# Fixing the order of the first heads phase of a graph network kernel, with two tap steps a block

## The chip, the core and the metric

The kernel runs on one core of one Trainium2 chip. The metric is the device time of one execution in microseconds (us); lower is better. The engines of the core are TensorE (PE in the profile; its weight loads are PEld), VectorE (DVE), ScalarE (ACT), GpSimd (POOL) and SyncE (SP). SyncE and ScalarE issue DMA transfers, each through a queue of its own.

## The reference

The input x has 128 graphs of 128 nodes and 256 channels, and a 0/1 adjacency matrix for each graph. All is float32. Layer 0 normalises and clips each node, and then has two branches: a pair of convolutions along the nodes, and a message passing step. A gated unit joins them. Layer 1 works on 25 nodes and is not touched by the change. Cut to what matters here:

```python
h = maximum(layernorm(x), 0)
xc = transpose(h)                             # channels x nodes
g = relu(bn1(conv1(xc)))                      # 1 tap: a product with a 256 x 256 matrix
g = bn2(conv2(g))                             # 17 taps along the nodes, 256 x 256 each
x_conv = relu(g + xc)
x_nmp  = (exp(-dist) * adj) @ relu(h @ w_msg.T + b_msg)
x = x + gated_unit(concat(x_conv, x_nmp), h)  # w_ih, w_hh
x = x + layer1(x, adj)                        # five small graph convolutions
```

## The kernel before, in words

The 17-tap convolution is done in the frequency domain. Nodes are cut into two windows of 80 samples; a window has 40 complex frequencies (`NP_`), with the first one holding two real ones. The graphs are worked on in blocks of four (`BB`), 16 blocks to a half, two halves (`NH`). The program has these phases:

1. **Heads of the first half.** Per block: `head_load` brings four graphs (tile `ln`, 512 KB). `head_stats` computes mean and variance on VectorE and the power -1/2 on GpSimd (L192, tile `rs`). `head_norm` normalises on VectorE (L198). `head_turn` transposes on TensorE (L208), clips on ScalarE into `ht` (L209) and stores `ht` for later (L210). `head_conv1` is the one-tap convolution (L222), an add on VectorE (L225) and a clip on ScalarE (L226) into `h1`. `head_spectra` transforms to frequencies (L237); VectorE and ScalarE put the result into the large tile `X` (L243, L245).
2. **Spectra of the taps**, woven into phase 1. `weight_spectra` transforms the taps of 128 input by 64 output channels at a time. There are eight such chunks, each of four *steps* (32 steps in all). A step has 16 small matmuls (L160, 17 rows, 80 columns) into four banks; ScalarE empties three and VectorE one (L168, L166), in the last step of a chunk ScalarE all four. When a chunk is done its 2.5 MB are stored to `vd` (L170), and the taps of the next but one are loaded (L150). `some_spectra(k)` does k steps; it is called twice in each block of `heads`.
3. **Frequencies of the first half** (`spectral`). Frequencies are worked on one after another. A tile `v` with the spectra of two frequencies is loaded from `vd` (L287, three buffers). GpSimd makes the sum `vs` of real and imaginary part (L302, three buffers), TensorE does three products in each frequency (L305, L314; L295 for the first), VectorE and ScalarE combine them into `ys`, which goes to `yd` (L318).
4. **Heads and frequencies of the second half.** The heads' beginning (`heads_begin`: loads, stats, norms and a turn) is called eight frequencies before the end of phase 3.
5. **Everything else** (L394 on), blocks of four graphs again: messages, inverse transform, gated unit, layer 1.

Three things set the order of the work. [...] That order is chosen by the framework's planner, which takes ready instructions by its own model of time and may move an instruction far ahead of its place in the text. Where a block of text stands under `manual_schedule`, the instructions of the named engines (of all, when none is named) keep the order of the text. The kernel before has no such block. It has two tricks that hold the planner back: a one-element-per-row copy from `h1` into the tile of the stats (L185), which ties the stats to the block before, and three one-column copies from `k1` into the tiles of the gate weights (L311), which keep the gate weights behind frequency 20.

PSUM, the accumulator of TensorE, has eight banks of 128 x 512, and all phases take their banks in turn from one pool (`bank`).

The weights of the gated unit (`wih`, `whh`), those of the messages (`wms`, `bms`), `idm` and `fw` are loaded in the text behind phase 3, 2.7 MB in all, and `gate_weights` makes twelve sums of them on GpSimd (L333 to L336).

## Time and profile before

The time before is 1971.03 us (median of three runs, 1967.3 to 1971.71). The profiled execution has a span of 1965.5 us.

| Engine | busy, us | share of the span | instructions |
|---|---|---|---|
| PE (matmuls) | 1910.6 | 97% | 10418 |
| PEld (weight loads) | 1666.5 | 85% | 10418 |
| DVE | 1279.2 | 65% | 3247 |
| ACT | 714.1 | 36% | 1472 |
| POOL | 610.0 | 31% | 684 |

The mean granted clock of TensorE is 0.983 of full speed; full speed is given as 1.00 in the views by window. By phase, from the views by window:

| Phase | from, us | to, us | granted clock | DMA share |
|---|---|---|---|---|
| start, to the first one-tap convolution | 0 | 21.9 | 0.95 | 0.85 |
| first heads, with tap steps | 21.9 | 133.6 | 0.78 | 0.71 |
| first heads, without | 133.6 | 211.7 | 0.93 | 0.61 |
| first frequencies | 211.7 | 321.4 | 0.98 | 0.83 |
| second heads | 321.4 | 427.4 | 1.00 | 0.45 |
| second frequencies | 427.4 | 529.7 | 1.00 | 0.85 |
| everything else | 529.7 | 1965 | 1.00 | 0.35 |

In lines of the profile, `out<-in` names the tile written and those read, `xN` counts instructions, and what stands in square brackets is the time for which the engine sat idle just before, with the instruction or transfer whose end released it. One fp32 matmul of the program gives two records.

### The profile page before, as it was taken

To read this page: it belongs to the slowest core of one execution; us is meant where nothing else is said; L and a number is where in the kernel's file an instruction comes from. 1 tells how busy PE (TensorE), PEld (TensorE's weight loads), DVE (VectorE), ACT (ScalarE), POOL (GpSimd) and SP (SyncE) were. 2 spreads that over 40 slices of the span, in tenths; PEclk is the share of its full clock that TensorE was granted. 3 is DMA by queue.
4 is the path that set the end of the run, shared out by engine and by line. 5 is a ranking of instruction groups with operands and counts; after the bars stand their busy time and mean duration, and the time that the engine had idled before them with its cause. 6 is when DMAs were issued, how large, how long until landed. Compare 5 with 4: busy or idle time off the path is not lost.

```text
span 1965.5 us, 29935 instructions
## 1 busy us (share of the span) xinstructions
PE 1910.6 (97%) x10418; PEld 1666.5 (85%) x10418; DVE 1279.2 (65%) x3247; ACT 714.1 (36%) x1472; POOL 610.0 (31%) x684
## 2 busy tenths in 40 slices
PE   7997999999989999999999999999999999999998
PEld 6887878998878888888878888888878888888887
DVE  5346545765478777777756677777756677777643
ACT  4443212431133333433434433333334434333334
POOL 1002363114423343344322143343322143343300
PEclk9788999999999999999999999999999999999999
DMA  8665688439863323323423533322423533322135
GB/s 325 262 268 192 221 267 299 152 122 304 281 203 83 94 70 85 91 68 81 121 61 100 127 104 89 90 71 72 126 71 91 130 94 97 82 71 61 46 91 148
DMA packets 248853, 265.76 MB, mean 135 GB/s; under 512 B 106850, under 2 KB 223927, under 8 KB 244223
## 3 DMA queue, kind: packets, MB, share of 16 engines
q1 hardware_dynamic: 236767, 196.74, 35.7%
q10 hardware_dynamic: 11936, 67.11, 8.5%
q8 instruction: 83, 1.36, 0.3%
q14 instruction: 67, 0.55, 0.1%
HBM read 178.66 MB, written 85.14 MB: 134 GB/s over the span
## 4 chain that ended last, share of the span: by engine, by line
PE 89%; DMA 4%; DVE 3%; POOL 1%; ACT 1%; issue 1%; SPq 0%; ACTq 0%; POOLq 0%; DVEq 0%
PE bank L572 44%; PE bank L314 7%; PE bank L478 5%; PE bank L222 5%; PE bank L891 5%; PE bank L831 5%; PE bank L305 3%; PE bank L237 3%; PE bank L460 3%; PE bank L524 3%; PE bank L463 1%; PE bank L511 1%; PE bank L810 1%; PE bank L742 1%; PE bank L208 1%; DVE st L187 1%
## 5 line engine op out<-in xcount | busy, mean ns | idle before, releaser
L572 PE MATMUL bank<-t,sw 128*128 128x256 f32 x1152 | 290.7, 379 | 0.0
L585 POOL TENSOR_TENSOR u<-u,m 128x256 f32<-128x256 f32 x128 | 92.7, 724 | 594.8 <-ACT m L583 536.2
L572 PEld LDWEIGHTS bank<-t,sw 128*128 128x128 f32 x1152 | 215.5, 190 | 29.6 <-issue 2.3
L572 PE MATMUL bank<-t,wih 128*128 128x256 f32 x768 | 197.2, 379 | 0.0
L572 PEld LDWEIGHTS bank<-t,wih 128*128 128x128 f32 x768 | 143.4, 190 | 19.3 <-DVE u L590 0.5
L302 POOL TENSOR_TENSOR vs<-v 128x512 f32<-128x512 f32 x78 | 101.1, 1315 | 141.3 <-DMA v<-vd 99.2
L222 PE MATMUL bank<-wc,ht 128*128 128x256 f32 x512 | 128.7, 408 | 12.8 <-ACT ht L209 11.4
L222 PEld LDWEIGHTS bank<-wc,ht 128*128 128x128 f32 x512 | 104.2, 208 | 29.8 <-ACT ht L209 12.9
L478 PE MATMUL bank<-wms,ht 128*128 128x259 f32 x512 | 122.3, 381 | 0.0
L300 DVE SCALAR_TENSOR_TENSOR s<-X 128x256 f32<-128x256 f32 x78 | 51.8, 666 | 98.9 <-PE bank L314 98.5
L572 PE MATMUL bank<-t,whh 128*128 128x256 f32 x384 | 114.4, 379 | 0.0
L891 PE MATMUL bank<-w,hh 128*125 128x256 f32 (+9 forms) x480 | 113.5, 380 | 0.9 <-DVE hh L836 0.9
L572 PE MATMUL bank<-xn,wih 128*128 128x256 f32 x384 | 114.2, 379 | 0.0
L572 PE MATMUL bank<-xc,wih 128*128 128x256 f32 x384 | 114.2, 379 | 0.0
L572 PE MATMUL bank<-ht,whh 128*128 128x256 f32 x384 | 109.8, 379 | 0.0
L478 PEld LDWEIGHTS bank<-wms,ht 128*128 128x128 f32 x512 | 97.2, 190 | 14.6
L831 PE MATMUL bank<-ax,w 128*128 128x500 f32 (+8 forms) x416 | 107.0, 396 | 0.4 <-DMA w<-in_w_dram 0.4
L192 POOL TENSOR_TENSOR rs<-ve,mhalf 128x4 f32<-128x4 f32 x32 | 32.3, 1008 | 232.0 <-DVE ve L190 232.0
L590 DVE TENSOR_TENSOR u<-bank,u 128x256 f32<-128x256 f32 x128 | 53.7, 420 | 73.5 <-PE bank L572 73.5
L482 ACT ACTIVATE msg<-msg 128x512 f32<-128x512 f32 x64 | 40.3, 630 | 167.4 <-DVE msg L479 162.0
L891 PEld LDWEIGHTS bank<-w,hh 128*125 128x125 f32 (+9 forms) x480 | 84.3, 178 | 19.1 <-DVE hh L836 1.3
L237 PE MATMUL bank<-fd,h 128*128 128x160 f32 x512 | 85.3, 323 | 8.4 <-DVE X L243 3.7
(192 smaller groups left out, 4255.2 us busy)
## 6 DMA issues: line engine op xcount, KB each, us to landing
v<-vd SPq DMA_DIRECT2D x80, 512.0 KB
vd<-sp ACTq DMA_DIRECT2D x8, 2560.0 KB
yd<-ys ACTq DMA_DIRECT2D x40, 512.0 KB
w<-in_w_dram SPq DMA_DIRECT2D x40, 512.0 KB
htd<-ht ACTq DMA_DIRECT2D x32, 512.0 KB
ht<-htd SPq DMA_DIRECT2D x32, 512.0 KB
ym<-yd SPq DMA_DIRECT2D x32, 512.0 KB
xt<-in_xT_dram SPq DMA_DIRECT2D x32, 512.0 KB
```

The source lines that it names most:

```text
L222: nc.tensor.matmul(pv[:, bb, :], ht[:, c, b * N:(b + 1) * N], wc1[:, c, :], start=c == 0, stop=c == C - 1)
L237: nc.tensor.matmul(ps[:, bb * 2 * LW:(bb + 1) * 2 * LW], h1[:, 2 * h + bb, c * P:(c + 1) * P], fd, start=True, stop=True)
L302: nc.gpsimd.tensor_tensor(vs, vr, vi, op=ALU.add)
L305: nc.tensor.matmul(p1[:, :D], a[:, c], vs[:, c], start=c == 0, stop=c == C - 1)
L314: nc.tensor.matmul(ps[:, k * D:(k + 1) * D], u[:, c], w[:, c], start=c == 0, stop=c == C - 1)
L460: nc.tensor.matmul(ps[:, b * N:(b + 1) * N], ym[:, b, o * P:(o + 1) * P], idm, start=b == 0, stop=False)
L478: nc.tensor.matmul(ps[:, :D + 3], ht[:, c, b * N:(b + 1) * N], wms[:, c, :], start=c == 0, stop=c == C - 1)
L524: nc.tensor.matmul(ps[:, b * N:(b + 1) * N], msg[:, b, c * P:(c + 1) * P], e[:, b, :], start=True, stop=True)
L572: nc.tensor.matmul(ps, w, d, start=n == 0, stop=n == len(pairs) - 1)
L585: nc.gpsimd.tensor_tensor(got["u4"], got["u2"], got["m5"], op=ALU.add)
L831: nc.tensor.matmul(pv[:, q - q0, :], w1s[k5 + g][:, c, q * P:(q + 1) * P], xv[:, c], start=c == 0, stop=c == C - 1)
L891: nc.tensor.matmul(ps[:n1, :D], hh[:, q, at:at + n1], w2s[k5 + g][:, q, :], start=q == 0, stop=q == HID // P - 1)
```

## The change

The heads of the first half, with the tap steps, get the order of the text on every engine (`ws.enter_context(tc.manual_schedule())`). SyncE and GpSimd get it from there to the end of the frequency phases (`order`, closed behind the loop over the halves). To suit this, the text is put in the order in which it is to run: the loads of the constants are split off, the start is written out with five tap steps in it, `heads_begin` serves the second half only, and `heads` does one tap step at each of its two places instead of two, so that the steps spread over some 14 blocks instead of seven. The stats of the first half are no longer tied to `h1`, and the copies of L311 are gone. The loads of the gate's weights go to frequency 4 of the first half (`gate_loads`) and the gate sums to frequency 20 (`NP_ // 2`); both stand in the text in front of that frequency's own instructions.

```diff
@@ heads @@
             if i + 3 < i1:
-                head_stats(wk, i + 3, h1s[i])
-
-    def spectral(bp, X, h, near_end):
+                head_stats(wk, i + 3, h1s[i] if h else None)
+
+    def spectral(bp, X, h, amid):
 
         for p0 in range(0, NP_, 4):
-            if p0 == NP_ - 8:
-                near_end()
+            amid.get(p0, lambda: None)()
...
-                if h == 0 and p == NP_ // 2:
-
-                    for t in sw:
-                        nc.gpsimd.tensor_copy(t[:, 0, 1, 0:1], k1[:, 0:1])
...
+        order = es.enter_context(ExitStack())
+        order.enter_context(tc.manual_schedule(engines={nc.sync.engine, nc.gpsimd.engine}))
         with ExitStack() as ws:
+
+            ws.enter_context(tc.manual_schedule())
...
-            taps = [taps_load(wp, *todo[k], nc.sync, split=1 if k else 4) for k in range(2)]
-            head_stats(hk, 0)
-            head_norm(0)
+            taps = [taps_load(wp, *todo[0], nc.sync, split=4)]
...
-            some_spectra(3)
+            constant_loads()
+            head_load(xk, ahead, 1, nc.sync)
+            taps.append(taps_load(wp, *todo[1], nc.sync))
+            for k in range(2, ahead):
+                head_load(xk, ahead, k, nc.sync)
+            head_stats(hk, 0)
+            some_spectra()
+            head_norm(0)
+            some_spectra()
+            head_turn(hk, 0)
             constants()
-            heads_begin(hk, xk, ahead, 0)
-            some_spectra(3)
-            heads(hk, xk, ahead, X, 0, lambda: some_spectra(2))
+            some_spectra()
+            head_stats(hk, 1)
+            some_spectra()
+            head_norm(1)
+            head_stats(hk, 2)
+            some_spectra()
+            heads(hk, xk, ahead, X, 0, some_spectra)
             while spectra or todo:
                 some_spectra()
...
+        def gate_loads():
+            nc.sync.dma_start(idm, io["idm"])
+            nc.sync.dma_start(wms, io["wms"].rearrange("(c p) o -> p c o", p=P))
+            nc.sync.dma_start(bms, row("bms", D + 3))
+            nc.sync.dma_start(fw, row("fw", 5))
+            nc.sync.dma_start(wih, io["wih"].rearrange("(c p) o -> p c o", p=P))
+            nc.sync.dma_start(whh, io["whh"].rearrange("(c p) o -> p c o", p=P))
+
+        amid = {4: gate_loads, NP_ // 2: gate_weights, NP_ - 8: lambda: heads_begin(hk, xk, 3, 1)}
         for h in range(NH):
             if h:
                 heads(hk, xk, 3, X, h, lambda: None)
-            spectral(bp, X, h, lambda: heads_begin(hk, xk, 3, h + 1) if h + 1 < NH else None)
-            if h == 0:
...
-                gate_weights()
+            spectral(bp, X, h, {} if h else amid)
+        order.close()
```

More of the change, by code (lines that the diff above doesn't have):

```diff
@@ L112, in gnn_kernel, with constant_loads @@
     brz = cst.tile([P, 4], F32)
-    def constants():
+    def constant_loads():
         nc.sync.dma_start(vec, io["vec"])
@@ L117, in constants @@
         nc.sync.dma_start(fd, io["fd"])
+    def constants():
         for j, v0 in enumerate((V_BN1, V_BN2)):
@@ L249, in heads_begin @@
         i = h * NBH
-        for k in range(1 if h == 0 else 0, ahead):
-            head_load(xk, ahead, i + k, nc.scalar if h else nc.sync)
-        for k in range(1 if h == 0 else 0, 3):
+        for k in range(ahead):
+            head_load(xk, ahead, i + k, nc.scalar)
+        for k in range(3):
             head_stats(wk, i + k)
@@ L383, in gnn_kernel @@
                 heads(hk, xk, 3, X, h, lambda: None)
-            spectral(bp, X, h, lambda: heads_begin(hk, xk, 3, h + 1) if h + 1 < NH else None)
-            if h == 0:
-                nc.sync.dma_start(idm, io["idm"])
-                nc.sync.dma_start(wms, io["wms"].rearrange("(c p) o -> p c o", p=P))
-                nc.sync.dma_start(bms, row("bms", D + 3))
-                nc.sync.dma_start(fw, row("fw", 5))
-                nc.sync.dma_start(wih, io["wih"].rearrange("(c p) o -> p c o", p=P))
-                nc.sync.dma_start(whh, io["whh"].rearrange("(c p) o -> p c o", p=P))
-                gate_weights()
+            spectral(bp, X, h, {} if h else amid)
+        order.close()
     wk = ctx.enter_context(tc.tile_pool(name="wk", bufs=1, reuse_waits="tile"))
```

## The prediction

> **What bounds the kernel now.** I read the page first. Its chain of waits gives 89% of the span to TensorE (PE), so a gain must come from PE idling or running slowly. Section 2 has the granted clock below 9 tenths only in its first slices, and PE's busy digits dip there too. So I cut the span by phase with the windows view (columns: busy us and instruction counts of PE, weight loads, VectorE (DVE), ScalarE (ACT) and GpSimd (POOL), then clock, DMA share, GB/s).
>
> ```profile
> 0.00:21.90 21.90, 13.06 (x208) 12.45 (x208) 11.32 (x48) 9.80 (x23) 4.53 (x14) 0.95 0.85 275
> 21.90:133.60 111.70, 99.26 (x1080) 85.78 (x1081) 46.71 (x149) 48.76 (x137) 7.04 (x7) 0.78 0.71 280
> 133.60:211.70 78.10, 64.71 (x386) 59.01 (x384) 53.44 (x189) 30.81 (x90) 13.90 (x13) 0.93 0.61 218
> 211.70:321.40 109.70, 105.57 (x484) 92.38 (x485) 49.20 (x79) 15.99 (x42) 59.37 (x52) 0.98 0.83 275
> 321.40:427.40 106.00, 104.64 (x636) 96.24 (x636) 76.39 (x266) 48.97 (x139) 16.69 (x16) 1.00 0.45 157
> ```
>
> The first half's heads end at 211.7 us. The second half's heads, the same work without tap steps, take 106.0 us at full clock. The tap steps (L160) explain part of the difference: in the timeline two of them (64 records) take 2.03 us at full clock, so 32 are worth 32 x 1.02 = 32 us. 106 + 32 + about 20 for the start is 158; some 53 us are lost. The PE timeline shows where:
>
> ```profile
> 96.79 2.03 PE L160 MATMUL bank<-gt,w 17*128 17x80 f32 x64
> 98.86 1.09 PE L208 MATMUL bank<-ident,ln 128*128 128x128 f32 x8
> 99.89 3.05 PE L160 MATMUL bank<-gt,w 17*128 17x80 f32 x64
> 103.96 1.53 PE L237 MATMUL bank<-fd,h 128*128 128x160 f32 x8 [1.03 <-DVE sp L166]
> 106.24 2.47 PE L237 MATMUL bank<-fd,h 128*128 128x160 f32 x8 [0.75 <-DVE X L243]
> 108.51 5.26 PE L222 MATMUL bank<-wc,ht 128*128 128x256 f32 x16
> ...
> 159.46 5.04 PE L222 MATMUL bank<-wc,ht 128*128 128x256 f32 x14 [10.08 <-ACT ht L209]
> ...
> 170.83 1.04 PE L208 MATMUL bank<-ident,ln 128*128 128x128 f32 x8
> 171.71 2.34 PE L237 MATMUL bank<-fd,h 128*128 128x160 f32 x16
> 173.88 3.62 PE L222 MATMUL bank<-wc,ht 128*128 128x256 f32 x16
> ...
> 282.55 2.08 PE L305 MATMUL bank<-vs,X 128*128 128x256 f32 x4 [4.10 <-POOL vs L302]
> ```
>
> A block with four steps takes 16.9 us (96.79 to 113.70); a bare block 6.50 (170.83 to 177.34: L208 0.87, L237 2.17, L222 3.45 by starts). Four steps add 4.1, so 6.3 us a block are lost: L237 and L222 run slowly, and two gaps. The clock explains the slowness:
>
> ```profile
> 98.17:101.58 3.41, 3.37 (x70) 3.01 (x66) 2.35 (x10) 3.38 (x11) 0.50 (x1) 1.00 0.11 8
> 101.58:105.00 3.42, 2.35 (x35) 2.04 (x35) 2.18 (x6) 1.49 (x6) 0.51 (x1) 1.00 0.97 372
> 105.00:108.41 3.41, 2.66 (x11) 2.29 (x10) 0.56 (x2) 1.68 (x7) 0.00 (x0) 0.50 1.05 450
> ```
>
> After a stretch of steps and transposes the clock is halved for two such windows. ACT is also full in the first one (3.38 of 3.41 us): it empties three of a step's four banks. The second loss is the 10.08 us gap at 159.46. Its cause stands in POOL's timeline:
>
> ```profile
> 134.90 1.01 POOL L192 TENSOR_TENSOR rs<-ve,mhalf 128x4 f32<-128x4 f32 x1 [15.90 <-DVE ve L190]
> 154.98 1.26 POOL L302 TENSOR_TENSOR vs<-v 128x512 f32<-128x512 f32 x1 [19.07 <-DMA v<-vd]
> 156.19 1.02 POOL L192 TENSOR_TENSOR rs<-ve,mhalf 128x4 f32<-128x4 f32 x1
> ```
>
> The next phase's first sum (L302) stood ahead of a head's power (L192) in POOL's queue and waited 19 us for spectra that were still being stored; the norm, transpose and convolution of that head waited behind it.
>
> [...] every spell of half clock is a multiple of 3.41 us. [...] rows x columns / 128 of the matmul records that start in a window (L160 10.6, L208 128, L237 160, L222 256; sixteen L222 make 4096). Windows that lost the clock had 1247, 1396 and 1556 (from 84.52, 101.58, 118.65); ones that kept it 1513 and 1597 (from 115.24, 98.17). [...]
>
> **The change part by part.**
>
> *Two steps a block, text order.* A block becomes L222, step, L208, step, L237. Its activity is 4096 + 1024 + 2560 + 64 x 10.6 = 8,360 units. Step, transpose, step last 1.02 + 0.87 + 1.02 = 2.9 us, shorter than a window, and hold 1,700 units by themselves: the clock stays whole. PE's floor is 6.50 + 2.04 = 8.5 us. The others have room: DVE two adds 1.3, two bank copies 0.9, norm 1.4, X copies 1.1, stats 2.3: 7.0; ACT two ReLUs 1.2, 6.25 copies at 0.35 are 2.2, two transposes' ReLUs 1.2, X copies 1.0, DMA issues 0.6: 6.2. Laying these out in text order against the eight banks, I find one wait: ACT does L226 first, which stands behind DVE's stats, so step two gets its banks some 0.5 us late. I take 9.1 us a block (bounds 8.6 and 10.5). Removing the copy that ties stats to h1 (L185, 0.2 us) is inside this.
>
> *DMA in this stretch.* Two blocks move 2.56 MB of spectra, 1 MB of taps and 2 x 1 MB of input and ht: 5.6 MB in 18.2 us, 305 GB/s. The trace reaches 450. A tap load goes out behind a 2.56 MB store and has four steps, 18 us, until it is used; 13.4 us were seen for it in the chain. Hidden, with little to spare.
>
> *Start.* Constants in text order put a serial chain on DVE (POOL's two powers at 0.7 each), but five steps instead of six precede the first L222, and vec is issued before the second tap tile. Before it started at 22.1; I take 21, at half clock (5.3 us), as before.
>
> *Sum of the heads.* 21; block 0 without L237 8.3 gives 29.3; twelve blocks at 9.1 give 138.5; block 13 with one step 7.7; block 14 6.5; block 15 5.6; last L237 2.2; X copies 1: 161.5. Before 211.7: **50 us less**. The last store of spectra goes out near 146, lands 9.7 later (chain of before) and the first v 3 us after that, 159: just hidden. POOL's order takes L302 out of the way of L192.
>
> *Gate loads at p = 4.* 2.7 MB, which before ran at 166 to 205 where DMA was idle, now stand between v loads on SyncE, and the second half's three inputs (1.5 MB) fall in the same stretch. v takes 1 MB per two frequencies and yd 0.5: 1.5 MB per 5.18 us, 300 GB/s[...]. From 156 the queue has 0.5 + 1 + 2.7 + 1 MB, plus up to 1.5, before the third v tile is there: 15 to 20 us, 171 to 176, plus the 1.3 us of L302; PE wants it near 173. Cost 0 to 6, I take 3 and, for one window of half clock, 1.5.
>
> *Gate weights at p = 20.* Twelve POOL operations in one piece: eight took 272.10 to 280.29, 1.02 each, so 12.3, plus L302 1.3. POOL is about 8.5 us ahead there (three vs buffers, 2.59 us a frequency): PE waits 5.1 against 4.10 before, each with a window of half clock. Cost 1 (bounds 0 and 5).
>
> *The rest* (SyncE and POOL in text order in the second heads and second frequency phase; the one-element copies L311 gone) I cost at nothing: there v's loads already followed the inputs, PE is 100% busy, and the next phase's loads began only after the last v at 516.
>
> **Sum.** 1971.0 - 50 + 4.5 + 1 = 1926.5; I say **1927 us**.
>
> **Rivals.** (a) *Banks or taps bind*: ACT's in-order work delays each second step by 2 us more, or taps come late. Block 10.9, 12 x 1.8 = 22 less gain: 1949. For it: ACT was full in the window above; against: it then had four steps' copies, now two. (b) *The clock still drops*: half of today's 6.3 us for half of the steps, 3.2 us a block, 12 x 3.2 = 38, and 5 more at start and end: 1970, no change. Against: 1,700 units in 2.9 us. (c) *Slower*: as (b), and the frequency phase becomes DMA-bound[...] and the POOL piece 5 more: about 1984. For it: DMA's share is 0.92 to 0.96 in slices of that phase. Against: the v tiles prefetch ahead.
>
> **How the numbers follow.** Forecast 0.68, (a) 0.18, (b) 0.05, (c) 0.06, and 0.03 for a still larger gain (block 8.6, nothing given back: 1915 or less). The range 1908 to 1955 holds the forecast and (a), and leaves (b) and (c) out. Faster 0.90: forecast, (a), the larger gain and a sliver of (b); same 0.04; slower 0.06.
>
> **What would show it.** Right: blocks near 9 us with clock 1.00 from about 28 us on, no POOL L302 among the L192 of the first half, frequency phase starting near 162, lasting 112 to 118, a PE gap of about 5 us at a POOL piece of twelve. Wrong: half clock recurring between 30 and 150, PE idle before L160 on ACT sp or on tap DMA, or PE waits on vs by v's DMA in many places.

## The result and the profile after

The changed kernel takes 1946.61 us (median of four runs, 1941.89 to 1952.97) against 1971.37 for the kernel before in the same comparison (1967.3 to 1971.94). The ratio is 0.9881, 95% interval 0.9848 to 0.9914: faster clear of the noise, by about 25 us (1.2%) and not by 44. The profiled execution has a span of 1942.6 us.

First the span by phase, in the view by windows of the changed kernel (columns as before). Its phases begin at 21.0, 168.5, 296.4, 402.1 and 504.9.

```profile
0.00:21.00 21.00, 12.92 (x176) 11.92 (x176) 9.41 (x36) 7.73 (x17) 3.88 (x14) 1.00 0.86 295
21.00:168.50 147.50, 143.51 (x1500) 126.18 (x1497) 100.50 (x317) 80.49 (x217) 16.11 (x16) 1.00 0.83 297
168.50:296.40 127.90, 109.62 (x484) 93.93 (x485) 58.54 (x109) 16.19 (x43) 63.43 (x53) 0.93 0.79 256
296.40:402.10 105.70, 104.33 (x634) 95.69 (x634) 78.67 (x264) 48.88 (x139) 16.88 (x16) 1.00 0.53 175
402.10:504.90 102.80, 102.80 (x478) 90.35 (x478) 47.64 (x79) 15.11 (x41) 47.12 (x39) 1.00 0.84 280
```

From 24.8, where the profile's clock record begins, the first heads run at full clock to their end, and PE is busy for 143.5 of their 147.5 us. (Their first convolution, at 21.04, took 5.57 us, later ones 3.62.) They end at 168.5 instead of 211.7. But the first frequency phase now takes 127.9 us where it took 109.7: PE has the same work there and idles for 18 us, and the clock fell to 0.93. So 43 us came in and 18 went back. The three phases behind it (105.6, 102.8 and 1437.8 us) are within 2 us of before (105.4, 102.9, 1435.8).

The PE timeline of the changed kernel, one block of the heads (the one-tap convolution is now L223, the transposes L209, the spectra L238, the steps L162):

```profile
48.96 3.62 PE L223 MATMUL bank<-wc,ht 128*128 128x256 f32 x16
52.50 1.13 PE L162 MATMUL bank<-gt,w 17*128 17x80 f32 x32
53.57 1.09 PE L209 MATMUL bank<-ident,ln 128*128 128x128 f32 x8
54.59 1.18 PE L162 MATMUL bank<-gt,w 17*128 17x80 f32 x32
55.70 2.44 PE L238 MATMUL bank<-fd,h 128*128 128x160 f32 x16
57.98 0.38 PE L223 MATMUL bank<-wc,ht 128*128 128x256 f32 x1
```

It is 9.02 us long (48.96 to 57.98) with no gap in it. Blocks of 9.0 and 9.8 us alternate; in the longer ones the first step stops after four of its 32 records until DVE's second add (L226) of that block is done, at 62.38 in the next block. The step takes 1.9 us there (61.53 to 63.43) instead of 1.1. What the first frequency phase lost stands in three places of the same timeline (L295 is the first frequency, L305 and L310 the products of the others):

```profile
164.43 0.81 PE L238 MATMUL bank<-fd,h 128*128 128x160 f32 x4 [1.27 <-ACT h L227]
166.13 1.90 PE L238 MATMUL bank<-fd,h 128*128 128x160 f32 x12 [0.90 <-ACT h L227]
...
173.02 2.90 PE L295 MATMUL bank<-v,X 128*128 128x256 f32 x6 [3.40 <-issue]
...
226.42 1.03 PE L310 MATMUL bank<-v,X 128*128 128x256 f32 x4
236.59 2.08 PE L305 MATMUL bank<-vs,X 128*128 128x256 f32 x4 [9.15 <-POOL vs L302]
...
275.25 1.10 PE L305 MATMUL bank<-vs,X 128*128 128x256 f32 x4 [3.02 <-DVE ys L311]
```

Two waits on `vs`, of 1.2 and 1.4 us, are the rest of the 18 us. After each of the two larger gaps the first matmuls are slow: the clock is halved for 6.8 us from 171.6 and for 10.2 us from 229.6, the only such spells before the last phase. DVE's timeline explains the first place:

```profile
162.69 0.43 DVE L188 BATCH_NORM_STATS2 st<-ln 128x6 f32<-128x256 f32 x1 [4.56 <-DMA ln<-in_x_dram]
163.04 0.67 DVE L226 TENSOR_TENSOR h<-bank,bnr 128x512 f32<-128x512 f32 x1
...
172.04 0.43 DVE L188 BATCH_NORM_STATS2 st<-ln 128x6 f32<-128x256 f32 x1 [3.37 <-DMA ln<-in_x_dram]
172.38 0.54 DVE L244 COPY X<-bank 128x160 f32<-128x160 f32 x2
```

Stats of the *second* half (L188) stand in DVE's queue ahead of the last block's add (L226) and of its last copies into `X` (L244), and wait for inputs that were only issued at 155 to 164. Under the planner, which still orders DVE behind the heads, they had moved up from frequency 32. The chain of waits has "DMA ln<-in_x_dram" for 7.27 us at 155.40. POOL's timeline has the second place:

```profile
167.21 1.27 POOL L302 TENSOR_TENSOR vs<-v 128x512 f32<-128x512 f32 x1 [19.82 <-DMA v<-vd]
...
219.90 2.49 POOL L302 TENSOR_TENSOR vs<-v 128x512 f32<-128x512 f32 x2 [2.99 <-DMA v<-vd]
222.35 1.18 POOL L329 TENSOR_TENSOR sw<-wih 128x384 f32<-128x384 f32 x1
...
234.33 0.99 POOL L332 TENSOR_TENSOR sw<-whh,sw 128x384 f32<-128x384 f32 x1
235.28 4.92 POOL L302 TENSOR_TENSOR vs<-v 128x512 f32<-128x512 f32 x4
```

The first line is the wait that used to stand in front of a head's power. It is still 19.8 us long, but nothing is queued behind it. The twelve gate sums run from 222.35 to 235.28 in one piece. PE had sums `vs` for 5 us more (to 227.4), then it waited. The third place is DVE's again: norms of the second half, ahead of the combining of `ys` (L311), waited for POOL's power (5.7 us to 265.6, 0.9 to 269.9). Three of them then began together with a sum `vs` on POOL and took 1.35 us each instead of 0.41, as in e2 below.

### The profile page after: what moved, and what is told of

Its sections match the earlier page's. It is cut to its first block, busy times and chain, and to the rows that moved or that the text cites. A ratio compares the mean times of both kernels' runs of the same rounds, so it can differ in the third digit from the quotient of the medians.

```text
span 1942.6 us, 29909 instructions
## 1 busy us (share of the span) xinstructions
PE 1897.4 (98%) x10418; PEld 1652.1 (85%) x10418; DVE 1288.1 (66%) x3247; ACT 713.2 (37%) x1459; POOL 608.8 (31%) x681
## 4 chain that ended last, share of the span: by engine, by line
PE 89%; DVE 4%; DMA 3%; POOL 2%; issue 1%; SPq 0%; ACT 0%; POOLq 0%; DVEq 0%; ACTq 0%
PE bank L586 43%; PE bank L310 5%; PE bank L492 5%; PE bank L905 5%; PE bank L845 5%; PE bank L223 4%; PE bank L238 3%; PE bank L538 3%; PE bank L474 3%; PE bank L305 3%; PE bank L162 2%; PE bank L477 1%; PE bank L525 1%; DMA v<-vd 1%; PE bank L209 1%; PE bank L824 1%
## 5 line engine op out<-in xcount | busy, mean ns | idle before, releaser
L223 PE MATMUL bank<-wc,ht 128*128 128x256 f32 x512 | 118.6, 385 | 1.4 <-ACT ht L210 1.4
L223 PEld LDWEIGHTS bank<-wc,ht 128*128 128x128 f32 x512 | 96.6, 193 | 15.0 <-ACT ht L210 2.8
L193 POOL TENSOR_TENSOR rs<-ve,mhalf 128x4 f32<-128x4 f32 x32 | 32.3, 1011 | 208.9 <-DVE ve L191 208.9
L307 ACT COPY k<-bank 128x256 f32<-128x256 f32 x78 | 29.0, 372 | 185.6 <-PE bank L305 76.2
```

Source lines behind the costliest of these rows:

```text
L223: nc.tensor.matmul(pv[:, bb, :], ht[:, c, b * N:(b + 1) * N], wc1[:, c, :], start=c == 0, stop=c == C - 1)
```

## The experiments

In all of them a phase is measured as above, from the first one-tap convolution or frequency product to the next. The table has what is compared. Each ratio is to the kernel before as measured beside that run (medians 1968.5 to 1972.3 us), so ratios compare better than medians. The three columns of phases are of one profiled execution each. As e8 will show, the same text of the first heads can end 11 us later in one execution than in another, so a few us in these columns need a cause in the trace.

| kernel | median us (range) | ratio to before, interval | heads end at | first frequencies | second heads |
|---|---|---|---|---|---|
| before | 1971.37 | | 211.7 | 109.7 | 105.4 |
| changed | 1946.61 (1941.9–1953.0) | 0.9881 [0.9848, 0.9914] | 168.5 | 127.9 | 105.6 |
| e1 sums spread | 1939.36 (1938.1–1941.6) | 0.9840 [0.9820, 0.9860] | 169.3 | 118.8 | 105.6 |
| e2 gate in second heads | 1937.97 (1935.7–1949.7) | 0.9843 [0.9816, 0.9870] | 169.6 | 114.8 | 110.9 |
| e3 inputs later | 1945.92 (1943.5–1949.4) | 0.9873 [0.9852, 0.9895] | 169.6 | 132.9 | 105.6 |
| e7 both | 1937.02 (1933.0–1939.6) | 0.9826 [0.9804, 0.9848] | 165.2 | 116.3 | 110.9 |
| e4 four steps | 1957.67 (1951.2–1958.6) | 0.9926 [0.9906, 0.9947] | 188.2 | 122.6 | 105.6 |
| e5 planner in the heads | 1988.30 (1983.1–1989.4) | 1.0087 [1.0070, 1.0103] | 216.0 | 125.9 | 105.6 |
| e6 two queues alone | 1954.48 (1950.6–1956.3) | 0.9917 [0.9902, 0.9933] | 195.5 | 111.5 | 105.6 |
| e8 all spread | 1924.27 (1922.9–1935.5) | 0.9781 [0.9758, 0.9804] | 176.1 | 113.0 | 105.6 |
| e9 steps apart | 1942.00 (1940.6–1949.8) | 0.9860 [0.9837, 0.9882] | 169.1 | 124.8 | 105.6 |
| e12 sums behind a copy from `X` | 1942.76 (1937.0–1949.1) | 0.9860 [0.9823, 0.9897] | 180.1 | 114.6 | 113.8 |
| e13 sums behind the norms | 1935.81 (1931.2–1941.6) | 0.9817 [0.9792, 0.9843] | 180.2 | 114.9 | 105.6 |
| e10 spread, steps apart | 1923.08 (1919.3–1925.9) | 0.9758 [0.9736, 0.9779] | 164.4 | 110.6 | 105.6 |

### What the first frequency phase gives back

**e1: the gate sums one a frequency.** The twelve sums are no longer in one piece: from frequency 20 on, each frequency makes one.

```diff
             for p in range(p0, p0 + 4):
+                if h == 0 and p >= NP_ // 2:
+                    next(sums, None)
...
             tt(s3, a11, a21, op=ALU.subtract)
+            yield
...
-        amid = {4: gate_loads, NP_ // 2: gate_weights, NP_ - 8: lambda: heads_begin(hk, xk, 3, 1)}
+        sums = gate_weights()
+        amid = {4: gate_loads, NP_ - 8: lambda: heads_begin(hk, xk, 3, 1)}
```

> The twelve gate sums one to a frequency from 20 to 31 instead of in one piece at 20; the loads stay at 4. Theory A (the piece itself stops PE for 9.2 us and costs a cold window): the first frequency phase falls from 127.5 to 114 to 117 us, no PE wait on vs over 2 us behind frequency 20, about 1934 us. Rival R (v's transfers are late anyway, the piece only covers it): the phase falls by less than 4 us, 1943 us or more.

Measured: the 9.15 us gap and the half clock behind it are gone, and the phase is 118.8 instead of 127.9 us, a little over the theory's 114 to 117. So the piece of twelve cost 9.1 us: the gap, less small waits that stay (up to 2.7 us), and the slow matmuls behind it. The half clock at the phase's start stays (6.8 us from 172.7), and one of 3.4 us comes at 258.0. The total is 1939.36, 7.3 us less, where the theory had about 1934. The second frequencies took 106.0 us in the profiled execution instead of 102.8, with one wait of 2.2 us for `vs`.

**e2: gate loads and gate sums out of the phase.** The loads stand behind the first half's `v` loads, the sums in the second half's heads, one at each of the two places of a block.

```diff
-        amid = {4: gate_loads, NP_ // 2: gate_weights, NP_ - 8: lambda: heads_begin(hk, xk, 3, 1)}
+        sums = gate_weights()
+        amid = {NP_ - 8: lambda: heads_begin(hk, xk, 3, 1)}
...
             if h:
-                heads(hk, xk, 3, X, h, lambda: None)
+                gate_loads()
+                heads(hk, xk, 3, X, h, lambda: next(sums, None))
```

> Gate loads behind the first half's frequencies on SyncE, the twelve sums one at a time in the second half's heads. Theory A: as spreading alone, and 1 to 4 us more where the loads stood between v's: first frequency phase 111 to 115, second heads longer by at most 1, 1930 to 1934 us. Rival R (the transfers bind): over 8 us better than spreading alone, 1926 us or less.

Measured: the phase is 114.8 us, 4.0 less than with the sums spread; that much at most is what the loads at frequency 4 cost, since e1 also had the half clock at 258.0, worth up to 1.7 us (half of its 3.4). But the second heads went from 105.6 to 110.9, where the theory allowed 1 us, and the total is that of e1. Blocks with sums take up to 7.7 us there instead of 6.5, with PE waiting for `ht`. POOL itself isn't late: its power (L193) still waits 4.64 us for DVE in such a block. DVE is. First the same norms in DVE's timeline of the changed kernel, then DVE's of e2, then POOL's of e2:

```profile
321.54 1.38 DVE L199 TENSOR_SCALAR ln<-ln,mv,rs 128x256 f32<-128x256 f32 x4 [1.12 <-POOL rs L193]
```

```profile
319.82 2.80 DVE L199 TENSOR_SCALAR ln<-ln,mv,rs 128x256 f32<-128x256 f32 x4 [1.12 <-POOL rs L193]
```

```profile
319.76 1.00 POOL L329 TENSOR_TENSOR sw<-whh 128x384 f32<-128x384 f32 x1
320.83 0.99 POOL L331 TENSOR_TENSOR whh<-whh 128x384 f32<-128x384 f32 x1
```

The four norms of a block together take twice as long while the two sums run: 2.80 us instead of 1.38. By single records, the two norms that begin together with a sum (within 0.07 us) take 1.08 and 1.15 us and end 0.15 us behind that sum, the other two 0.40 us each as usual, and the sums keep their 1.0 us. The sums start when the power is done, and so do the norms: the place was an unlucky one. What holds the norms up there isn't shown; two later runs, e12 and e13, test whether it is the meeting.

**e3: the second half's inputs later**, loaded by SyncE at frequency 16 and not by ACT's queue.

```diff
-        for k in range(ahead):
-            head_load(xk, ahead, i + k, nc.scalar)
...
-        amid = {4: gate_loads, NP_ // 2: gate_weights, NP_ - 8: lambda: heads_begin(hk, xk, 3, 1)}
+        amid = {4: gate_loads, NP_ // 2: gate_weights, 16: lambda: [head_load(xk, 3, NBH + k, nc.sync) for k in range(3)],
+                NP_ - 8: lambda: heads_begin(hk, xk, 3, 1)}
```

> Only the second half's first three inputs moved: from ScalarE's queue, where the planner issues them at 155 us, to SyncE's at frequency 16. Theory A (VectorE's stats of these inputs stand ahead of the last block's h1 and X copies and wait for the transfer): the first L295 comes 3 to 4 us earlier (about 165), the gap of 3.4 us behind it goes, 1937 to 1940 us. Rival R (the end of the heads waits for the last spectra and v): first L295 stays near 168, 1945 us or more.

Measured: the total, 1945.92, is no better than the changed kernel's, and the heads end at 169.6, as the rival had it. Yet the theory was right about the end of the heads: from the last convolution's start to the first frequency product it now takes 7.8 us instead of 11.2, so the stats are gone from there. It doesn't show in the heads' end, because this execution lost the clock twice among the steps (3.4 us each at 85.0 and 105.5, two blocks of 11.4 us instead of 9.8), and its block 0 was 1.0 us longer. In the first frequency another operation has taken the stats' place. DVE's timeline of e3, then PE's:

```profile
168.67 0.56 DVE L244 COPY X<-bank 128x160 f32<-128x160 f32 x2 [0.53 <-PE bank L238]
176.18 0.16 DVE L438 TENSOR_REDUCE fmx<-fw 128x1 f32<-128x5 f32 x1 [6.96 <-DMA fw<-in_fw_dram]
...
176.51 0.55 DVE L244 COPY X<-bank 128x160 f32<-128x160 f32 x2
```

```profile
177.16 2.90 PE L293 MATMUL bank<-v,X 128*128 128x256 f32 x6 [5.23 <-ACT fex L442]
```

A reduction over the five weights `fw` of a later phase (loaded with the gate's) stands before the last copies into `X` and waits 7 us for its small load, which is queued on SyncE behind `v`. PE waits 5.2 us for those copies (the view names ACT's `fex`, but the matmul reads `X`, whose copy ended at 177.06), and the phase takes 132.9 us. An early load lets the planner bring its reader forward; there were two such loads here, and one taken away left the other.

**e7: e2 and e3 together.** Its edit is the sum of theirs.

> Inputs late and gate loads and sums in the second heads, together. Theory A: the two savings add, first frequency phase 106 to 110 from about 165 us, 1922 to 1927 us. Rival R: no better than the better of the two alone.

Measured: the heads end at 165.2 (the last block's convolution starts at 157.4 in both this and the changed kernel, so the blocked DVE cost 3.3 us there), and the 3.4 us gap in the first frequency is gone. But the total, 1937.02, is no better than e2's, as the rival had it and not the theory, and the first frequencies take 116.3 us. The second heads still lose 5.3 us to the sums. `v` comes 3.7 us late once, at 207; three inputs were issued at once ahead of it, which I take to be the cause. A wait of 3.0 us on DVE's norms, as at 275 in the changed kernel, comes at 255, with 6.8 us of half clock.

**e12 and e13: the sums of e2 at another moment of the block.** In both, six blocks make two sums each, and a one-element copy on POOL in front of the two reads something that is written late. In e12 that is `X`, in e13 the last column that the block's norms write. The edit of e12 on e2, and that of e13 on e12:

```diff
-                heads(hk, xk, 3, X, h, lambda: next(sums, None))
+                heads(hk, xk, 3, X, h, two_sums)
...
+        def two_sums():
...
+            if odd or not 2 <= n < 8:
+                return
...
+            nc.gpsimd.tensor_copy(sw[k][:, 0, j, 0:1], X[:, C - 1, NP_ - 1, 1, HG + (n - 2) * BB:HG + (n - 2) * BB + 1])
+            next(sums)
+            next(sums)
```

```diff
-            if odd or not 2 <= n < 8:
+            if not odd or not 2 <= n < 8:
...
-            nc.gpsimd.tensor_copy(sw[k][:, 0, j, 0:1], X[:, C - 1, NP_ - 1, 1, HG + (n - 2) * BB:HG + (n - 2) * BB + 1])
+            nc.gpsimd.tensor_copy(sw[k][:, 0, j, 0:1], xs[NBH + n + 2][:, BB - 1, D - 1:D])
```

> The run with the gate loads and sums in the second heads, changed in one point: in six of its blocks the two sums stand behind a one-element copy from X, which lets them start when ScalarE has written its last spectra of that block, some 1.3 us after the power, when the block's norms on VectorE are done. Theory [...]: the norms of these blocks take 1.4 us again and not 2.8, no PE wait on ht in blocks with sums but for the first two, second heads 105.5 to 107.0 instead of 110.9, total 1932 to 1937. Rival (it is the sums' place in GpSimd's queue, or their traffic, whatever VectorE does at that moment): second heads 109 to 112 as before, norms long or not, total 1936 to 1942.

> The run before it missed its aim: the element of X had been written before the power was done, so the sums still began together with the norms, and six blocks with sums instead of five had norms of 2.93 us and cost 8.2 us instead of 5.3. Now the one-element copy reads the last column that the block's last norm writes, so that the two sums begin when the norms end; their number, their order and the blocks are the same. Theory [...]: all norms 1.4 us, sums from 1.4 to 3.6 us behind the power's end, the blocks 6.5 us, second heads 105.5 to 107.0. Rival (sums on GpSimd cost the second heads what they cost wherever in the block they stand): second heads 111 to 115. The heads of the first half can end anywhere from 168 to 181[...], so that the total, 1931 to 1945, tells nothing here.

Measured: in e12 the sums still began together with the norms, as the expectation of e13 says, and its second heads took 113.8. In e13 they took 105.6, as in the changed kernel without any sums there. DVE's timeline of e13, then POOL's:

```profile
320.19 1.38 DVE L199 TENSOR_SCALAR ln<-ln,mv,rs 128x256 f32<-128x256 f32 x4 [1.13 <-POOL rs L193]
```

```profile
321.64 0.18 POOL L414 COPY sw<-ln 128x1 f32<-128x1 f32 x1 [1.48 <-DVE ln L199]
321.78 1.00 POOL L333 TENSOR_TENSOR sw<-wih 128x384 f32<-128x384 f32 x1
322.86 1.00 POOL L335 TENSOR_TENSOR sw<-wih,sw 128x384 f32<-128x384 f32 x1
```

The same sums 1.5 us later cost nothing: it was the meeting with the norms. (In the profiled executions of both runs the first heads lost the clock three times, as in the next run.)

**e8: everything apart.** Inputs at three frequencies with their stats and norms at others, gate loads behind `v`, gate sums one a frequency from frequency 8 of the second half's *frequencies*, where POOL has time.

```diff
+                if h and p >= 8:
+                    next(sums, None)
...
+        def second(k):
+            head_load(xk, 3, NBH + k, nc.sync)
+
+        def more():
+            head_stats(hk, NBH + 1)
+            head_norm(NBH)
+
+        def last():
+            head_stats(hk, NBH + 2)
+            head_norm(NBH + 1)
+            head_turn(hk, NBH)
+
+        amid = {12: lambda: second(0), 16: lambda: second(1), 20: lambda: head_stats(hk, NBH),
+                24: lambda: [second(2), more()], NP_ - 8: last}
...
+                gate_loads()
                 heads(hk, xk, 3, X, h, lambda: None)
```

> The changed kernel with all that was added to the first frequency phase spread or moved: the second half's inputs loaded by SyncE at frequencies 12, 16 and 24, their statistics and norms apart from each other, the gate loads behind the first half's v loads, the gate sums one a frequency from frequency 8 of the second half. Theory (the give-back is waits and cold clock made by pieces that stand in one lump, and each can be hidden): first frequency phase 105 to 111 from about 165, second heads 105 to 107, second frequency phase 102 to 106, total 1915 to 1927. Rival (the transfers of v bind whatever else stands there): first phase 114 or more and the second phase 106 or more, total 1930 or more, no better than with the gate sums in the second heads.

Measured: 1924.27, inside what the theory gave for the total. The second heads (105.6) and second frequencies (103.1, with the sums in them) are as they should be. The first frequencies took 113.0, between the two theories' numbers. The heads are a surprise: in the profiled execution, which took 1935.5 us where the four others took 1922.9 to 1929.4, they end at 176.1 (165.2 in e7), with half clock for 6.8 us at 47.2, 88.1 and 129.1. Their text is that of the changed kernel. The PE timeline and the view by windows, cut where the granted clock changed at 47.16 and at steps of 3.41 us from there, show where:

```profile
43.69 0.65 PE L162 MATMUL bank<-gt,w 17*128 17x80 f32 x4
44.54 1.12 PE L162 MATMUL bank<-gt,w 17*128 17x80 f32 x28 [0.21 <-DVE h L226]
45.59 1.09 PE L209 MATMUL bank<-ident,ln 128*128 128x128 f32 x8
46.62 1.56 PE L162 MATMUL bank<-gt,w 17*128 17x80 f32 x32
48.11 4.63 PE L238 MATMUL bank<-fd,h 128*128 128x160 f32 x16
```

```profile
40.33:43.75 3.42, 3.42 (x17) 2.73 (x16) 3.24 (x12) 1.38 (x6) 0.37 (x1) 1.00 1.07 443
43.75:47.16 3.41, 3.20 (x61) 2.81 (x60) 2.16 (x7) 2.92 (x7) 0.64 (x1) 1.00 1.21 417
47.16:50.57 3.41, 3.41 (x33) 3.27 (x26) 0.85 (x3) 1.99 (x6) 0.00 (x0) 0.50 0.79 246
```

The spells of half clock read here last whole multiples of 3.41 us (6.8 in e8, 6.8 and 10.2 in the changed kernel), so I call a stretch of 3.41 us that ends at such a step a window. The one from 43.75 to 47.16 lies on step, transpose, step. PE is busy 3.20 of 3.41 us in it, and it holds 1565 units (rows x columns / 128 of the matmul records that start in it, as the prediction counts). The next window is at half clock. In the changed kernel's profiled execution no window between 28 and 157 held less than 1660. Eight kernels here have this text of the first heads. In their profiled executions the changed kernel, e1, e2 and e7 kept the clock among the steps, e3 lost it twice, and e8, e12 and e13 three times; so the text alone doesn't set whether the clock is lost. In e8 the losses come 40.9 and 41.0 us apart: four blocks with a spell in them take 41.0 us (40.14 to 81.12), and so do twelve times 3.41. That one loss brings the next in this way, by putting a window on the same place, is an inference.

### What gives the 43 us in the heads

**e4: four steps a block again**, all else as in the changed kernel.

```diff
-            heads(hk, xk, ahead, X, 0, some_spectra)
+            heads(hk, xk, ahead, X, 0, lambda: some_spectra(2))
```

> The changed kernel with four tap steps a block instead of two, everything else (text order on every engine, early loads) kept. It asks whether the gain in the heads is from the spreading of the steps or from the order. Theory (the spreading keeps PE's clock): stretches of step, step, transpose, step, step last 5 us again [...], so the half clock comes back in most of the seven blocks with four steps, these last 15 to 17.5 us, the bare ones 6.5 to 7.5; the heads end 12 to 30 us later than in the changed kernel (180 to 198 instead of 168.5), total 1955 to 1975. Rival (the order of the text alone gave the gain): clock 1.00 between 30 and 160 as in the changed kernel, heads end within 4 us of 168.5, total 1943 to 1950.

Measured: heads end at 188.2, total 1957.67: both in the theory's range. Between 30 and 160 there are five spells of half clock, and the blocks with four steps take 12.2 to 16.2 us. PE also waited for taps (5.5 us in three waits, the longest 2.60 at 107.21), which four steps a block use up faster. The spreading is worth 20 us in these two executions; how much of that is the clock and how much the taps isn't separated.

**e5: two steps, but the planner's order on PE, DVE and ACT.** Its stats aren't tied to `h1` either, as in the changed kernel.

```diff
-            ws.enter_context(tc.manual_schedule())
```

> The changed kernel with two tap steps a block, but the order of PE, DVE and ACT in the first half's heads left to the planner again (SyncE and GpSimd stay in text order). Theory (what counts is two steps a block and GpSimd's order): the planner keeps PE's steps apart in the main, half clock in at most three windows between 30 and 160, heads end within 6 us of 168.5, total 1940 to 1952. Rival (the hand order of PE, DVE and ACT is what gives the 43 us): the planner bunches steps where it finds room, half clock in six or more windows, heads end at 180 or later, total 1955 to 1972.

Measured: 1988.30, slower than the kernel before. The theory that two steps and GpSimd's order are enough fell, and the rival's numbers were too mild. The timelines of e5, PE and then DVE:

```profile
76.10 1.12 PE L162 MATMUL bank<-gt,w 17*128 17x80 f32 x16
78.65 2.40 PE L162 MATMUL bank<-gt,w 17*128 17x80 f32 x16 [1.43 <-DVE h L226]
80.99 1.97 PE L209 MATMUL bank<-ident,ln 128*128 128x128 f32 x8
82.88 2.01 PE L162 MATMUL bank<-gt,w 17*128 17x80 f32 x32
84.83 4.63 PE L238 MATMUL bank<-fd,h 128*128 128x160 f32 x16
```

```profile
75.34 0.69 DVE L226 TENSOR_TENSOR h<-bank,bnr 128x512 f32<-128x512 f32 x1
76.62 1.38 DVE L199 TENSOR_SCALAR ln<-ln,mv,rs 128x256 f32<-128x256 f32 x4 [0.59 <-POOL rs L193]
77.91 0.69 DVE L226 TENSOR_TENSOR h<-bank,bnr 128x512 f32<-128x512 f32 x1
```

The planner put a norm (L199) between the two adds of a convolution. It waits 0.6 us for POOL's power and takes 1.4; the second add, a bank and PE's step come that much later. The 1.43 us that PE stands still lie among the steps, and what follows runs slowly: the transposes take 1.97 us instead of 1.09 (at 94.02 in the same trace), the second step 2.01 instead of 1.13 (a step at 92.95) and the spectra 4.63 instead of 2.44 (at 70.28). From the third block on every second one is 14 to 17 us long, the others 9 to 10. Here two steps a block paid only with an order that leaves no such gap between them. Whether the tie of the stats to `h1`, which the kernel before has, would have kept the planner from this isn't tested.

**e6: the kernel before with text order on SyncE and GpSimd alone.** The copies of L311 are gone, the gate sums stand one a frequency in the second half's.

```diff
+        order = es.enter_context(ExitStack())
+        order.enter_context(tc.manual_schedule(engines={nc.sync.engine, nc.gpsimd.engine}))
...
-                if h == 0 and p == NP_ // 2:
...
-                gate_weights()
+                sums = gate_weights()
+        order.close()
```

> The kernel before with one part of the change alone: SyncE and GpSimd in text order to the end of the frequency phases (one-element copies gone, gate loads behind the first half's frequencies as before, gate sums one a frequency in the second half's). Four steps a block, planner's order on the other engines. Theory: only the 10 us gap at 149 to 159 goes, where a frequency sum stood ahead of a head's power on GpSimd; the half clock in the heads stays (six or more spells); heads end at 199 to 203 instead of 211.7, first frequency phase 108 to 113, total 1958 to 1964. Rival (the order of these two queues gives most of the 43 us in the heads): heads end at 180 or earlier, total 1935 to 1945.

Measured: heads end at 195.5, 4 us earlier than the theory's 199 to 203, total 1954.48, 3.5 better than its range. The gap at 149 to 159 is gone. POOL's timeline of e6 has the powers at work up to the last one, at 177.01, and `vs` right behind:

```profile
177.01 1.01 POOL L192 TENSOR_TENSOR rs<-ve,mhalf 128x4 f32<-128x4 f32 x1 [5.65 <-DVE ve L190]
177.99 3.82 POOL L304 TENSOR_TENSOR vs<-v 128x512 f32<-128x512 f32 x3
```

The theory counted only the gap of 10.1 us. By the starts of the convolutions its block took 18.6 us in the kernel before (148.8 to 167.4) where a bare one takes 6.5, so with the slow matmuls behind it the gap was worth 12.1; the way from the last convolution's start to the first frequency is 2.8 us shorter too (11.8 to 9.0). The blocks with steps end 3.1 us earlier (132.7 for 135.8), and the last block but one is 1.8 us longer. Five spells of half clock stay among the steps; the theory said six or more. So of the 43 us, 16 need nothing but the order of two queues. Order on the other engines, the untied stats and the new start give 7 more with four steps (e4, 188.2), and two steps a block 20 more. The parts hold for this order of adding, and each rests on one execution, with the clock's chance of up to 11 us in it.

### The clock's windows, and the best version

**e9: the two steps of a block apart**, convolution, step, transpose, spectra, step.

```diff
-            between()
             if i > i0:
                 head_spectra(X, i - 1)
+            between()
             if i + 3 < i1:
```

> The changed kernel with the second tap step of a block moved behind the spectra (L222-like convolution, step, transpose, spectra, step) so that the two steps are no longer 3 us apart with only a transpose between them. The kernel with everything spread lost the clock three times in its heads, in windows that held 1533 to 1565 units and lay on step, transpose, step, which there last 3.3 us and not the 2.9 I counted. Theory (whether a window falls on that stretch differs from execution to execution): with the steps apart no window between 30 and 165 holds less than 2,000 units, no half clock there, block 9.0 to 9.6, heads end at 166 to 170, total 1937 to 1947, and the executions lie closer together than the changed kernel's 11 us. Rival (the later step runs into banks that DVE and ACT have not emptied): blocks of 10 us or more with PE waiting on sp or X, heads end at 175 or later, total 1950 or more.

Measured: blocks of 9.0 and 9.7 us as before, no half clock between 28 and 160, and the emptiest window there, from 61.5, holds 2323 units where the changed kernel's, from 137.5, had 1660. (A window from 162.2, in the waits at the heads' end, held 1280 and lost the clock.) Total 1942.00. The half of the expectation on the clock held among the steps; that the executions would lie closer together did not (9.2 us from end to end, against 11.1): the spread has other sources as well, the frequency phase's gaps among them, and I didn't find which.

**e10: e8 with the steps apart**, and the third stats called at frequency 28.

```diff
-                24: lambda: [second(2), more()], NP_ - 8: last}
+                24: lambda: [second(2), more()], 28: lambda: head_stats(hk, NBH + 2), NP_ - 8: last}
```

> The kernel with everything spread, with two edits more: the two steps of a block apart as in the run beside it, and the third statistics of the second half called at frequency 28, so that their power stands eight frequencies earlier on GpSimd and the norm that DVE has already begun to wait for no longer holds it 5.5 us (PE gap 3.35 near frequency 31). Theory: no half clock in the heads, heads end at 166 to 172, first frequency phase 105 to 111, second heads 105 to 107, second frequencies 102 to 104, total 1910 to 1921 with executions within 8 us of each other. Rival (v's transfers bind in the first frequency phase whatever stands where): first phase 112 or more with gaps of PE on vs behind v, total 1922 or more.

Measured: 1923.08 (1919.3 to 1925.9), the best of all, if within e8's range. Phase by phase in the view by windows:

```profile
21.20:164.40 143.20, 141.87 (x1500) 123.50 (x1497) 98.07 (x301) 80.05 (x217) 14.77 (x15) 1.00 0.81 293
164.40:275.10 110.70, 104.87 (x487) 90.88 (x486) 60.71 (x124) 16.49 (x45) 52.92 (x42) 1.00 0.91 302
275.10:380.70 105.60, 104.24 (x634) 95.61 (x633) 78.63 (x264) 48.75 (x139) 16.88 (x16) 1.00 0.56 186
380.70:483.50 102.80, 102.80 (x479) 90.35 (x477) 50.45 (x79) 15.14 (x41) 59.60 (x51) 1.00 0.85 280
```

The clock is 1.00 in all four. The heads end at 164.4, and the first frequency phase is within 1 us of before at 110.6, so `v`'s transfers don't bind it, though DMA's share is now 0.91. One gap of 3.3 us is left in it, at 213.8: DVE again waits 5.5 us in a norm for POOL's power (of another head than in e8), and then two norms begin together with sums `vs` and take 1.35 us each instead of 0.40. It is the meeting of e2 once more. The twelve sums cost the second frequencies nothing. The median is 2 us above the expected range while the profiled execution (1919.3) lies inside.

## Why the prediction was right, and where it wasn't

The direction, the main mechanism and the range held; the size was off by 20 us (1946.6 against 1926.5). That the range held is in part luck: its upper part was there for rival (a), and what filled it was mostly another loss. By phase, on the profiled executions: heads 7.0 us, first frequencies 12.7 (127.9 against 109.7 + 5.5) and the rest 2.0 more than forecast. That is, to the rounding, the 21.6 us by which the span's change (1965.5 to 1942.6) stayed behind the forecast's 44.5.

- **Halved clock and a 10 us gap on POOL as what was lost.** Right. e4 shows the part of the spread steps (20 us, taps included), e6 that of the two queues (16).
- **A block of 9.1 us.** Measured 9.42 on average (9.02 and 9.82 in turn), and block 0 took 9.0 against 8.3: together 4.6 us of the heads' 7.0. A wait was foreseen for the second step, at 0.5 us in every block. It stands in the first step of every second block, behind DVE's add, and is worth 0.8; and a block with no wait at all takes 9.02 us, 0.5 over the floor of 8.5.
- **"Step, transpose, step last 2.9 us, shorter than a window: the clock stays whole."** True in the changed kernel's profiled execution, but not safe. Two of its four executions had a lower mean clock (0.989 against 0.992 and 0.993) and took 1948.8 and 1953.0 us; whether they lost it among the steps isn't known, since they have no trace. The stretch lasts 3.2 us in the shorter blocks (52.50 to 55.70) and 4.0 in the longer ones (61.53 to 65.52), against the 3.41 of a window, and e8 lost the clock behind three windows on it, of 1533 to 1565 units. That 1,700 units would keep the clock was the author's estimate, from five windows of the trace before. The count doesn't tell which windows keep it: in that trace 1556 lost the clock, and of two windows of 1513 the one from 115.24 kept it and the one from 64.04 lost it; in the changed kernel 1536, from 270.57, kept it.
- **The end of the heads, 8.8 us from the last convolution's start.** Measured 11.2; this is the first step that failed. Stats that the planner had moved up on DVE waited for inputs issued in that moment. e3, e7, e8 and e10, which load later, all have 7.8. The trace before had a warning: the same way took 11.8 us there, with DVE's norms and stats of the second half among the last copies (the wait of 1.89 us at 211.74 is on such a copy). The prediction priced those inputs as traffic for `v`, not as an invitation to the planner; the same wait reaches into the first frequency (3.4 us, and a slow clock behind it).
- **The first `v` "just hidden".** Right in the changed kernel, but by luck: `v` came at 167.2 and not at 159, and the first `vs` still started 1.8 us before PE used it because the heads ended late as well. In e7, e8 and e10 PE waited 0.8 to 1.2 us for it.
- **Gate loads and inputs 4.5 us.** e1 against e2 gives at most 4.0 for the loads. The 15 to 20 us for 5.2 to 6.7 MB were the author's estimate, some 340 GB/s; the windows view before shows 275 GB/s in that phase, at a DMA share of 0.83.
- **The gate sums, 1 us (bounds 0 and 5).** The term that was mis-sized: 9.1 us in e1. The twelve took 12.9 us, near the 12.3 worked out; but POOL was 5.1 us ahead when they began and not 8.5, since it had just waited 3.0 us for `v`. 12.9 + 1.3 - 5.1 is the 9.15 us gap, and the clock fell for 10.2 us where I allowed 3.4.
- **The rest at nothing.** Right for the second heads and frequencies: 0.2 and -0.1. (Second frequencies with the same text took 105.6 in e9's execution, so they vary too.) The last phase's 2.0 was not looked into; in the runs it varies from 1433.8 to 1437.8. One loss has no term: the 3.0 us at 275, where norms on DVE waited for POOL's power and then met POOL's sums.

Rival (a) had nearly the right time, 1949, for largely another reason: the longer blocks gave 4.6 us and taps nothing; most of the other 15 went back in the phase behind. Rival (b), the falling clock, is what e4 and e5 became.

## What to carry to other kernels

When a long phase gets shorter, look at what was put into the next one to make room: the lump of twelve sums on GpSimd cost its length less the engine's lead (a gap of 9.15 us) and then 10.2 us of half clock, while the same sums one at a time, where the engine has room, cost nothing measurable (second frequencies 102.8 us in e10 as in the changed kernel). Where a hand order ends and a planner takes over, an early load can let its readers move ahead of urgent work, and moving one such load leaves the next. Spreading the small matmuls paid here with waits of 0.2 us among them (changed kernel) and not with waits of 1.43 (e5, 1988.30 us); with the spectra between the two steps (e9, e10) no profiled execution lost the clock among them. Norms on VectorE are best kept from starting beside GpSimd's sums: four took 2.80 us there instead of 1.38 (e2).

## What the runs showed of the hardware

- A stretch that kept PE busy for 3.20 of 3.41 us, two thirds of that with 17-row matmuls, was followed by 6.8 us of half clock (e8, 43.75 to 47.16).
- The same instructions kept the clock in one execution and lost it in another: the first heads of e8, e12 and e13 have the changed kernel's text, and lost the clock three times each, in e8 41 us apart. Each time was 6.8 us of half clock, and the heads ended 10.5 to 10.9 us later than in e2 and e7, which end in the same way and kept the clock. In e8 the execution of 1935.5 us had a mean granted clock of 0.991, the four of 1922.9 to 1929.4 had 0.996 to 0.998. In e13 the two of 1931.2 and 1931.4 us had 0.995 and 0.996, those of 1940.2 and 1941.6 had 0.990 and 0.991. That the windows lie differently on the instructions from one execution to the next is an inference, since only one of each kernel has a trace.
- Waits of 1.3 to 1.5 us among the steps went with two or three windows of half clock each (e5, five times), and a block with one took 5.5 to 7.6 us more than the block behind it.
- A norm of DVE that began within 0.12 us of the start of a POOL sum ended 0.15 us behind that sum: 1.08 and 1.15 us instead of 0.41 beside sums of 1.0 us (e2), 1.35 beside sums of 1.3 us (changed kernel, 269.9 to 273.8). With DVE and POOL both idle for a part of each block, the meetings made the second heads 5.3 us longer (110.9 in e2 for 105.6); 1.5 us later the sums cost nothing (e13, 105.6).
